# Three changes of order in a two-layer graph kernel: later loads of x and of the diagonal, other ticks for the projections, scatters without pacing copies

## The chip, the core and the metric

The kernel runs on one core of one Trainium2 chip. Five engines share the work: TensorE (PE in the profile, its weight loads PEld), VectorE (DVE), ScalarE (ACT), GpSimd (POOL) and SyncE (SP, which issues most DMAs). Each engine [...]waits on semaphores of the others. The metric is the device time of one execution in microseconds (us); lower is better.

## What is computed

The input is a batch of 16 graphs of 1024 nodes with 128 features each, and a symmetric 0/1 adjacency. Layer 0 is a masked attention, layer 1 three rounds of a graph convolution on a thinned ("dilated") adjacency. Cut to what matters:

```python
h = jnp.maximum(_layernorm(x), 0)                    # layer 0
v, q, k = relu(h @ Wv.T + bv), relu(h @ Wq.T + bq), relu(h @ Wk.T + bk)
logits = (q @ k.T) * adj - NEG * (1 - adj)
x = x + relu((softmax(logits) @ v) @ Wo.T + bo)
h = jnp.maximum(_layernorm(x), 0)                    # layer 1
adj_d = _dilate(adj, nodemask)                       # row by row, each row's removals affect later rows
h1 = _bn(relu(_sage(h,  adj_d, Wr1, Wx1, b1)))       # _sage: (adj_d @ x / deg) @ Wr + x @ Wx + b, row-normalised
h2 = _bn(relu(_sage(h1, adj_d, Wr2, Wx2, b2)))       # _bn: statistics over all graphs and nodes
h3 = _bn(relu(_sage(h2, adj_d, Wr3, Wx3, b3)))
x = x + concat(h1, h2, h3) @ Wl + bl
```

## The kernel before, in words

**Attention stage.** One step for each of the 16 graphs. A step has 48 ticks (TICKS, L35); a tick is a little over 1 us. The function step(i) (L893) issues 16 score blocks of 128 x 512 (scores, L737: PE into PSUM tile ps, ScalarE's exp into e, VectorE's product with the adjacency), each followed by two pieces of the values of the half before (values, L750: PE into po). After each piece pace() (L876) moves the tick on and advances every generator in the agenda whose next due tick has come. So everything beside the scores and values has its place in each engine's queue by a list of ticks, written by hand and counted from the step's start; plan(gen, start, ticks) (L801) enters a generator in the agenda. Clock.later (L63) puts a piece of work a given number of ticks later.

In step i the agenda holds, among others:

- load_adj(i + 1) (L820, Dilation.load L164) at AT_LOAD, ticks 1, 4, 7 and so on: eight row blocks of the next adjacency, 512 KB each, by SP into one of three st buffers (L162); ScalarE turns each into a bf16 mask ab (L174) and counts its zeros (L191). A row block takes two of the ticks, so the blocks stand at ticks 1, 7, 13, ... in the queues. SP has nothing else to wait for and runs ahead of the ticks as soon as the st buffer of three blocks ago is free.
- project(i + 1) (L698) at AT_PROJECT (L780), a list for even and one for odd steps: moments of x (DVE and POOL), normalised rows hn (POOL, L617), transposes (PE, L627), Q, K, V (PE, L720, evicted by ScalarE at L721) and V times Wo (PE, L728, evicted by DVE). From the transposes on they all use one PSUM tile, pm, with a single buffer: each piece waits until ScalarE or DVE has emptied it of the piece before.
- in odd steps the sort and the two gathers of the dilation (ticks 27 to 47 for the most part); in groups of steps its solve.
- store(i - 1) (L769, L829) from tick 75 on, so in the step after the next boundary: eight scatters of 128 rows of the new x to DRAM by POOL (scatter, L571). Odd and even steps differ in when POOL comes to them.

Two things stand outside the agenda: at the head of step i the loop at L917 issues load_x(i + 2) (L691: 512 KB by SP at L695 into one of five xt buffers, and a small DVE copy at L696 into a column of the same buffer) and dil.read_diagonal(i) (L222: 1024 single elements by SP, used by the final verdict only). The xt buffer that load_x(i + 2) takes is that of graph i - 3, whose scatters were issued in step i - 1. In step 0 the loads are in the agenda (first_loads, L885).

**Layer 1.** Rounds one and two keep their results in SBUF (r1, r2). Round three (from L1305) computes for each graph a tile y of 1024 rows of 256 numbers: the round's output (mix, L1029) and the sum of the two earlier thirds with x (thirds, L1327, added by DVE at L1131). Five graphs (STAY: 2, 5, 8, 11, 14) stay in SBUF; the rows of the other eleven are scattered to DRAM by POOL in the order of the nodes (scatter_rows, L1337: eight scatters each, 88 in all) and read back by SP (load_back, L1321). y comes from a pool of three buffers (L1305); a buffer can be used again when its scatters have landed. The scatters wait in a list, and pace_scatters (L1295), called after each of the eight pieces of a graph, puts at most one of them into POOL's queue:

```python
if ticks3 % 6 and waiting and waiting[0][0] <= ticks3:
    if marked:
        nc.gpsimd.tensor_copy(mark, last[0])
    waiting.pop(0)[1]()
```

last[0] is one column of whatever DVE last had to write in program order (a norm, batch statistics, y or z), so a scatter doesn't start before DVE has come that far. The last stage (the final product and the output, from L1433 on) has marked off and uses the same pace_scatters for its 40 scatters of the output.

Of the kernel before, what the change touches and what calls it, by code (L numbers as in the profile page):

```python
# [16 lines left out]
B, N, D = 16, 1024, 128  # L17
# [17 lines left out]
TICKS = 6 * NB  # L35
# [14 lines left out]
def _advance(gen, n=1):  # L50
    for _ in range(n):
        if next(gen, gen) is gen:
            return False
    return True
# [491 lines left out]
def fast(ctx: ExitStack, tc: tile.TileContext, a, out, vp):  # L546
# [31 lines left out]
    def load_const(name, shape, src):  # L578
        t = consts.tile(shape, F32, name=name)
        nc.sync.dma_start(t, src)  # L580
        return t

    def column(name):
        return load_const("c_" + name, [P, 1], a[name].rearrange("(p o) -> p o", o=1))

    def row_all(name):
        ap = a[name]
        return load_const("r_" + name, [P, P], bass.AP(tensor=ap.tensor, offset=ap.offset, ap=[[0, P], [1, P]]))
# [94 lines left out]
    with ExitStack() as s1:  # L683
        att = s1.enter_context(tc.tile_pool(name="att", bufs=2))
        aps = s1.enter_context(tc.tile_pool(name="aps", bufs=2, space=PSUM))
        dil = Dilation(tc, adj, accT, kept, jp, identf, dpool, dpsum,
                       rows.enter_context(tc.tile_pool(name="adj", bufs=2, side="right")), aps, clock)
# [3 lines left out]
        def load_x(b):  # L691
            X[b] = xpool.tile([P, NB, XW], F32, name="xt")
            for k in range(0, NB, NB if b else NB // 2):
                k = slice(k, k + (NB if b else NB // 2))
                nc.sync.dma_start(X[b][:, k, :D], x_in[b].rearrange("(k p) d -> p k d", p=P)[:, k])  # L695
            nc.vector.tensor_copy(X[b][:, :, D].bitcast(I32), dil.node32)  # L696
# [40 lines left out]
        def scores(b, g, k):  # L737

            p = aps.tile([P, 512], F32, name="ps")
            c = slice(512 * g, 512 * g + 512)  # L740
            nc.tensor.matmul(p, K[b][:, k * P:(k + 1) * P], Q[b][:, c], start=True, stop=True)  # L741
            e = att.tile([P, 512], F32, name="e", bufs=16)
            later(1, lambda: nc.scalar.activation(e, p, AF.Exp))  # L743
            later(2, lambda: nc.vector.tensor_mul(e, e, AB_[b][:, k, c]))  # L744
            return e
# [4 lines left out]
        def values(b, g, E, i, part):  # L750

            q = 4 * g + i
            if q % 2 == 0 and part == 0:
                pairs[b] = aps.tile([P, 2, D + 1], F32, name="po")
            po = pairs[b]
            for k in range(2 * part, 2 * part + 2):
                nc.tensor.matmul(po[:, q % 2, :], E[k][:, i * P:(i + 1) * P], V[b][:, k, :], start=(k == 0),  # L757
                                 stop=(k == NB - 1))
            if part < 3 or q % 2 == 0:
                return  # L760
            o = att.tile([P, 2, D], F32, name="o")
            rec = recips[:, b, q - 1:q + 1]
            x = X[b][:, q - 1:q + 1, :D]
            later(1, lambda: nc.vector.reciprocal(rec, po[:, :, D]))  # L764
            for h in range(2):
                later(2 + h, lambda h=h: nc.scalar.activation(o[:, h, :], po[:, h, :D], AF.Relu, scale=rec[:, h:h + 1]))  # L766
            later(5, lambda: nc.vector.tensor_add(x, x, o))

        def store(b):  # L769
            for k in range(NB):  # L770
# [6 lines left out]

        every = lambda first, n, by: [first + by * j for j in range(n)]

        AT_PROJECT = [m + every(m[4] + hn, 4, 1) + every(m[4] + wait, 10, 3)  # L780
                      for m, hn, wait in (([1, 2, 4, 7, 13], 4, 17), ([0, 1, 3, 5, 6], 4, 18))]
        AT_LOAD = every(1, 2 * NB, 3)
        AT_BOUND = [[0] + [first + by * (j // 2) + j % 2 for j in range(2 * NB)] for first, by in ((2, 5), (3, 3))]
        AT_MIRRORS = ([5, 10, 20, 25, 30, 35, 40, 44], [13, 16, 19, 22, 25, 29, 33, 41])
# [16 lines left out]
        def plan(gen, start, ticks):  # L801
            agenda.append((gen, [start + t for t in ticks]))
# [4 lines left out]
        def plan_step(i):  # L807

            start, odd = i * TICKS, i % 2
            if i == 0:  # L810

                late = lambda ticks: [TICKS // 2 + t // 2 for t in ticks]
                plan(values0, start, [3, 6, 9, 12])
            else:
                late = lambda ticks: ticks
            plan(dil.bound(i), start, AT_BOUND[odd] if i else [25, 28, 29, 30, 31, 33, 34, 35, 36, 38, 39, 40, 41, 43, 44, 45, 46])
            plan(dil.mirrors(i), start, AT_MIRRORS[odd] if i else [6, 9, 12, 15, 18, 21, 25, 28])
            if i + 1 < B:
                plan(project(i + 1), start, AT_PROJECT[odd] if i else [14, 16, 18, 20, 21, 23, 24, 25, 26, 32, 34, 36, 38, 40, 42, 43, 45, 46, 47])
                plan(load_adj(i + 1), start, AT_LOAD if i else [23, 24, 25, 27, 28, 30, 31, 32, 34, 35, 37, 38, 39, 41, 42, 44])  # L820
            if odd:
                plan(dil.sort(i - 1), start, AT_SORT)
                for b, ticks in zip((i - 1, i), LAST_GATHER if i == B - 1 else AT_GATHER):
                    gathering[b] = dil.gather(b, spare if b == B - 2 else None)
                    plan(gathering[b], start, ticks)
            if i:
                last = i == B - 1
                plan(norms_of_x2(i - 1, att), start, LAST_NORMS if last else AT_NORMS[odd])
                plan(store(i - 1), start, LAST_STORE if last else AT_STORE)  # L829
            for b0, b1, t0, t1 in GROUPS:  # L830
                if t0 // TICKS == i:
                    n = solve_pieces(b0, b1)
                    plan(dil.solve(b0, b1), 0, [t0 + j * (t1 - t0) // n for j in range(n)])
# [3 lines left out]
        def load_adj(b):  # L837
            g = dil.load(b)
            next(g)
            AB_[b] = dil.A[b][0]  # L840
            yield
            yield from g
# [33 lines left out]
        def pace():  # L876
            nonlocal tick
            clock.tick()
            for gen, ticks in agenda:
                while ticks and ticks[0] <= tick:  # L880
                    ticks.pop(0)
                    _advance(gen)
            tick += 1

        def first_loads():  # L885
            load_x(1)
            yield
            load_x(2)
            yield
            dil.read_diagonal(0)  # L890
            yield

        def step(i):  # L893
            nonlocal prev
            if i == 0:
                plan(first_loads(), 0, [1, 20, 26])
            plan_step(i)
            for g in range(2):
                E = []
                for k in range(NB):  # L900
                    E.append(scores(i, g, k))
                    if i == 0 and g == 0:
                        _advance(first, 2)
                    pace()
                    for h in range(2):
                        if prev:
                            values(*prev, k // 2, k % 2 * 2 + h)
                        pace()
                prev = (i, g, E)
# [3 lines left out]
        def load_x2(b):  # L913
            XT[b] = xpool.tile([P, NB, XW], F32, name="xt")
            nc.sync.dma_start(XT[b], x2_d[b].rearrange("(k p) d -> p k d", p=P))

        for i in range(B):  # L917
            if 0 < i < B - 2:
                load_x(i + 2)
            if i == B - 1:  # L920
                load_x2(0)
                load_x2(1)
            if i:
                dil.read_diagonal(i)
            step(i)
            if i == 0:
                wr = [load_const(f"wr{k}", [P, P], a[f"L1_gnn_Wr{k}"]) for k in (1, 2, 3)]
                wx = [load_const(f"wx{k}", [P, P], a[f"L1_gnn_Wx{k}"]) for k in (1, 2, 3)]
                gs = [column(f"L1_gnn_g{k}") for k in (1, 2, 3)]
                bes = [column(f"L1_gnn_be{k}") for k in (1, 2, 3)]  # L930
                wl = load_const("wl", [P, 3, P], a["L1_gnn_Wl"].rearrange("(k p) e -> p k e", p=P))
                below, shares, place, cols = selectors()
                bs = [row_all(f"L1_gnn_b{k}") for k in (1, 2, 3)]
                bl = row_all("L1_gnn_bl")
                for r in bs + [bl]:
                    nc.vector.tensor_scalar(r, r, below[:, 0:1], None, op0=OP.mult)
# [294 lines left out]
    with big:  # L1231
# [58 lines left out]
        rows_r = lambda b: blocks(r2[b // 2][:, b % 2, :])  # L1290
        rows_z = lambda b: blocks(r1[b // 2][:, b % 2, :])
        mark = few.tile([P, 1], F32, name="mark")
        waiting, ticks3, marked = [], 0, True

        def pace_scatters():  # L1295

# [136 lines left out]
        marked = False  # L1433
# [591 lines left out]
```

## Time and profile before

| what | before |
|---|---|
| median of 3 runs | 1218.25 us (1217.69 to 1220.84) |
| profiled execution | 1223.52 us, span of the records 1221.7 us |
| PE busy, weight loads | 1067.6 us (87%), 826.8 us (68%) |
| DVE, ACT, POOL busy | 846.0 us (69%), 727.2 us (60%), 575.2 us (47%) |
| granted PE clock, mean | 0.961 |
| attention stage | about 20 to 768 us |
| round three | about 984 to 1132 us |
| last stage | about 1132 to 1222 us |
| mark copies (L1302) | 81, 0.20 us each |

How to read the profile: a line of the waits names the engine and line that waited, after the arrow what ended the wait, then the sum in us, how often, and the longest. A line of the timeline has start, duration, engine, line, operation, output and input tile, and in brackets the idle time of the engine just before, with what ended it; "remote" means that a semaphore ended it and no instruction that ended just then explains it. "issue" is time in which nothing is seen to be waited for. A letter q after an engine is its sequencer: for SPq, the time until a DMA was issued. Matmul records have modelled ends.

### The profile page before, as it was taken

How to read it: one execution, taken by the hardware profiler on the slowest of the kernel's cores; microseconds unless marked ns; L12 is line 12 of the kernel's file. 1: busy time of each engine (PE TensorE's matmuls, PEld its weight loads, DVE VectorE, ACT ScalarE, POOL GpSimd, SP SyncE). 2: the span in 40 equal slices, each digit the busy share in tenths (PEclk: the TensorE clock that was granted, in tenths of full speed). 3: DMA queues.
4: the chain of work that ended last, by engine and by line, in shares of the span. 5: the costliest groups of instructions: out<-in, count | busy, mean ns of one | idle time of the engine just before them, and what ended most of it. 6: DMA issues, size and time to landing. Idle time of an engine off the chain costs nothing.

```text
span 1221.7 us, 22431 instructions
## 1 busy us (share of the span) xinstructions
PE 1067.6 (87%) x7731; PEld 826.8 (68%) x7731; DVE 846.0 (69%) x2611; ACT 727.2 (60%) x1771; POOL 575.2 (47%) x1063
## 2 busy tenths in 40 slices
PE   8899989989989989989999998789779887878693
PEld 3567666766666766666666676678769877878583
DVE  7757647578867657867877988679878755556331
ACT  5677866877767767766777762468758522222120
POOL 0321742842733634554446344789401056665563
PEclk9999999999999999999999999899989999898796
DMA  7445244244344344344443421334000046665542
GB/s 233 128 145 141 86 141 145 93 141 139 99 128 140 111 131 124 119 122 118 116 131 105 126 84 38 106 82 114 19 18 1 3 145 199 186 194 164 164 144 84
DMA packets 135355, 143.77 MB, mean 118 GB/s; under 512 B 25920, under 2 KB 111296, under 8 KB 135232
## 3 DMA queue, kind: packets, MB, share of 16 engines
q1 hardware_dynamic: 123328, 111.10, 32.0%
q0 software_dynamic: 11904, 31.15, 7.8%
q8 instruction: 62, 1.02, 0.3%
q14 instruction: 61, 0.50, 0.1%
HBM read 113.71 MB, written 28.51 MB: 116 GB/s over the span
## 4 chain that ended last, share of the span: by engine, by line
PE 58%; DVE 16%; ACT 10%; issue 4%; POOL 4%; DMA 3%; another core or an unknown queue 3%; POOLq 0%; DVEq 0%; ACTq 0%
PE po L757 13%; PE ps L741 12%; PE pm L720 5%; PE po L1056 4%; PE po L1394 3%; DMA st<-in_adj_dram 3%; DVE e L744 2%; ACT e L743 2%; PE pt L1114 2%; PE pm L728 2%; PE pd L200 2%; POOL x_d L573 2%; PE pt L1332 2%; PE pt L1333 2%
## 5 line engine op out<-in xcount | busy, mean ns | idle before, releaser
L757 PEld LDWEIGHTS po<-vw,e 128*128 128x128 f32 x2048 | 270.8, 194 | 58.4 <-issue 58.2
L757 PE MATMUL po<-vw,e 128*128 128x129 f32 x2048 | 304.8, 284 | 0.0
L744 DVE TENSOR_TENSOR e<-e,ab 128x512 f32<-128x512 f32 x256 | 177.7, 694 | 156.6 <-ACT e L743 147.0
L741 PE MATMUL ps<-qT,kT 128*128 128x512 f32 x512 | 269.9, 609 | 0.6 <-ACT kT L721 0.6
L743 ACT ACTIVATE e<-ps 128x512 f32<-128x512 f32 x256 | 153.4, 600 | 94.7 <-PE ps L741 88.1
L174 ACT ACTIVATE ab<-st,d_one_k 128x1024 bf16<-128x1024 f32 x126 | 145.6, 1155 | 26.9 <-DMA st<-in_adj_dram 26.8
L573 POOL DMA_INDIRECT x_d<-xt,slot x128 | 142.9, 1116 | 39.3 <-issue 33.0
L191 ACT ACTIVATE junk<-st 128x1024 bf16<-128x1024 f32 x112 | 118.6, 1059 | 0.0
L313 POOL DMA_INDIRECT rows<-in_adj_dram,row x15 | 17.2, 1147 | 177.3 <-DVE junkv L206 82.1
L573 POOL DMA_INDIRECT y_d<-y,nodes x88 | 86.3, 981 | 22.5 <-issue 18.0
L605 POOL TENSOR_SCALAR ln_t<-ln_st 128x8 f32<-128x8 f32 x31 | 11.1, 357 | 177.4 <-DVE ln_st L598 172.2
L1072 ACT ACTIVATE sq<-po 128x512 f32<-128x512 f32 x48 | 28.5, 597 | 97.8 <-remote 39.3
L766 ACT ACTIVATE o<-po,recips 128x128 f32<-128x128 f32 x128 | 46.6, 367 | 64.1 <-DVE recips L764 59.4
L741 PEld LDWEIGHTS ps<-qT,kT 128*128 128x128 f32 x512 | 78.5, 193 | 3.6 <-ACT kT L721 1.7
L1056 PE MATMUL po<-ws,r 128*128 128x128 f32 x512 | 69.0, 277 | 3.7 <-issue 3.6
L1056 PEld LDWEIGHTS po<-ws,r 128*128 128x128 f32 x512 | 65.9, 194 | 6.3 <-issue 5.2
L617 POOL TENSOR_SCALAR hn<-xt,ln 128x128 f32<-128x128 f32 x120 | 65.0, 553 | 3.2 <-ACT e L743 1.1
L206 DVE SCALAR_TENSOR_TENSOR junkv<-pd,ab 128x64 bf16<-128x64 int32 (+7 forms) x128 | 57.4, 448 | 12.5 <-PE ps L741 6.7
L1332 PE MATMUL pt<-ws,r 128*128 128x128 f32 x224 | 48.6, 302 | 16.4 <-DVE y L1131 11.4
L728 PEld LDWEIGHTS pm<-w_L_gnn_Wo,hn 128*128 128x128 f32 x256 | 34.7, 201 | 35.2 <-ACT hn L721 22.1
L617 POOL TENSOR_SCALAR hn<-xt 128x128 f32<-128x128 f32 x112 | 54.4, 496 | 8.1 <-PE pt L627 7.2
L1131 DVE TENSOR_TENSOR r<-r,po 128x512 f32<-128x512 f32 x32 | 21.1, 685 | 52.5 <-remote 30.6
(346 smaller groups left out, 2485.5 us busy)
## 6 DMA issues: line engine op xcount, KB each, us to landing
st<-in_adj_dram SPq DMA_DIRECT2D x126, 512.0 KB
r<-y_d SPq DMA_DIRECT2D x22, 512.0 KB
xt<-x_d SPq DMA_DIRECT2D x16, 524.0 KB
x<-x_d SPq DMA_DIRECT2D x16, 512.0 KB
xt<-in_x_dram SPq DMA_DIRECT2D x15, 512.0 KB
out_dram<-r SPq DMA_DIRECT2D x11, 512.0 KB
x_d<-xt,slot POOLq DMA_INDIRECT x128
y_d<-y,nodes POOLq DMA_INDIRECT x88
```

What stands on the lines that cost most here:

```text
L174: nc.scalar.activation(ab[:, k, :], st, AF.Exp, bias=self.one_k, scale=ONE_K, accum_out=self.deg[:, b, k:k + 1])
L191: nc.scalar.activation(junk(), st, AF.Exp, scale=-ZERO_K, accum_out=zeros)
L573: d = nc.gpsimd.indirect_dma_start(out=dst, out_offset=bass.IndirectOffsetOnAxis(ap=slots, axis=0), in_=src, in_offset=None)
L617: engine.tensor_scalar(hn[:, k, :], xt[:, k, :D], minus[:, k // 2, k % 2, None], rstd[:, k // 2, k % 2, None], op0=OP.add, op1=OP.mult)
L720: nc.tensor.matmul(pp, w, hT[:, 512 * g:512 * g + 512], start=True, stop=True)
L728: nc.tensor.matmul(pp[:, k, :], vT[:, j * P:(j + 1) * P], wo, start=True, stop=True)
L741: nc.tensor.matmul(p, K[b][:, k * P:(k + 1) * P], Q[b][:, c], start=True, stop=True)
L743: later(1, lambda: nc.scalar.activation(e, p, AF.Exp))
L744: later(2, lambda: nc.vector.tensor_mul(e, e, AB_[b][:, k, c]))
L757: nc.tensor.matmul(po[:, q % 2, :], E[k][:, i * P:(i + 1) * P], V[b][:, k, :], start=(k == 0), stop=(k == NB - 1))
L1056: nc.tensor.matmul(po[:, i, :], hT[:, c:c + P], wxk, start=(i == 3), stop=False)
L1332: nc.tensor.matmul(pz[:, i, :], column(r1, b, g, i), wl0, start=True, stop=False)
```

## The change

Three edits, independent of each other.

1. load_x(i + 2) and read_diagonal(i) go from the head of the step into the agenda: a generator small_loads(i) at ticks 8 and 14 of every step from 1 on (step 0 keeps its ticks 1, 20, 26). At the last two steps, where there is no further x, tick 8 is empty.
2. AT_PROJECT spells its last ten ticks out. The list for even steps is the same as before (30, 33, ... 57). For odd steps it was 24, 27, 30, ... 51 and becomes 20, 23, 26, 29, 32, 42, 45, 48, 51, 54.
3. marked is False from the start, so round three's scatters go into POOL's queue without a copy into mark ahead of each; each waits for its own data alone.

```diff
-        AT_PROJECT = [m + every(m[4] + hn, 4, 1) + every(m[4] + wait, 10, 3)
-                      for m, hn, wait in (([1, 2, 4, 7, 13], 4, 17), ([0, 1, 3, 5, 6], 4, 18))]
+        AT_PROJECT = [m + every(m[4] + 4, 4, 1) + turned
+                      for m, turned in (([1, 2, 4, 7, 13], [30, 33, 36, 39, 42, 45, 48, 51, 54, 57]),
+                                        ([0, 1, 3, 5, 6], [20, 23, 26, 29, 32, 42, 45, 48, 51, 54]))]
...
-        def first_loads():
-            load_x(1)
-            yield
-            load_x(2)
-            yield
-            dil.read_diagonal(0)
+        def small_loads(i):
+            if i == 0:
+                load_x(1)
+                yield
+            if i + 2 < B:
+                load_x(i + 2)
+            yield
+            dil.read_diagonal(i)
             yield
 
         def step(i):
             nonlocal prev
-            if i == 0:
-                plan(first_loads(), 0, [1, 20, 26])
+            plan(small_loads(i), i * TICKS, [8, 14] if i else [1, 20, 26])
             plan_step(i)
...
         for i in range(B):
-            if 0 < i < B - 2:
-                load_x(i + 2)
             if i == B - 1:
                 load_x2(0)
                 load_x2(1)
-            if i:
-                dil.read_diagonal(i)
             step(i)
...
-        waiting, ticks3, marked = [], 0, True
+        waiting, ticks3, marked = [], 0, False
```

## The prediction, made before the result was known

> **What bounds the kernel now.** I read the waits of the attention stage first (60 to 760 us of the span), then busy time by attention step, then the timelines of one odd step's start and of one stretch of round three.
>
> Waits in 60 to 760 us (engine, line, whom it waited for: us, times, longest). First TensorE (PE), then ScalarE (ACT), then SP's own queue:
>
> ```profile
> PE pm L728 <- ACT hn L721: 16.0, 7, 3.1
> PE pm L720 <- ACT kT L721: 11.6, 10, 2.3
> PE pm L720 <- ACT qT L721: 5.4, 5, 1.5
> ```
> ```profile
> ACT ab L174 <- DMA st<-in_adj_dram: 20.5, 6, 4.1
> ```
> ```profile
> SPq L695 <- DMA x_d<-xt,slot: 78.8, 12, 17.3
> ```
>
> PE is the engine that the stage runs at; it loses 33 us to these three waits for the one-buffered PSUM tile pm, which ScalarE empties. ScalarE itself stands 20.5 us waiting for adjacency rows, and SP stands 78.8 us at the load of x, because that load overwrites a buffer that scatters of two steps ago still read. Steps 9, 10 and 11 (window, its length, PE, weight loads, DVE, ACT, POOL, clock, DMA share, GB/s):
>
> ```profile
> 436.50:486.00 49.50, 44.34 (x311) 30.71 (x310) 34.02 (x129) 34.88 (x68) 21.33 (x45) 0.97 0.48 138
> 486.00:532.30 46.30, 43.90 (x339) 31.81 (x338) 36.58 (x116) 34.07 (x70) 25.47 (x45) 1.00 0.34 104
> 532.30:584.50 52.20, 46.22 (x306) 33.07 (x306) 35.88 (x143) 34.93 (x69) 20.88 (x45) 0.93 0.48 133
> ```
>
> Odd steps are longer with about the same PE work. Steps 3, 5, 7, 9, 11, 13 take 49.1, 49.2, 50.7, 49.5, 52.2 and 47.3 us (298.0), steps 4 to 14 even take 44.6, 45.2, 44.5, 46.3, 46.6 and 45.1 (272.3): 25.7 us apart. Why, at the start of step 11: SP gets its load of x out at 530.79 (the scatters' last descriptors were written at 529.3), and only then the first rows of adjacency; ScalarE and PE stop:
>
> ```profile
> 530.79 0.38 SPq L695 DMA_DIRECT2D xt<-in_x_dram  x1
> ...
> 531.89 9.21 SPq L162 DMA_DIRECT2D st<-in_adj_dram  x4
> ```
> ```profile
> 537.41 1.15 ACT L174 ACTIVATE ab<-st,d_one_k 128x1024 bf16<-128x1024 f32 x1 [3.71 <-DMA st<-in_adj_dram]
> ```
> ```profile
> 539.76 1.87 PE L728 MATMUL pm<-w_L_gnn_Wo,hn 128*128 128x128 f32 x8 [3.01 <-ACT hn L721]
> ```
>
> Round three (about 984 to 1132 us) is bound otherwise. GpSimd (POOL) writes 88 scatters and ahead of 81 of them a copy into mark; VectorE (DVE) and ScalarE stop in bursts for 5 to 6 us, and each stop ends when POOL has run out of scatters:
>
> ```profile
> 1036.01 0.98 POOL L573 DMA_INDIRECT y_d<-y,nodes  x1 [0.16 <-issue]
> 1043.19 0.18 POOL L1302 COPY mark<-y 128x1 f32<-128x1 f32 x1 [6.20 <-DVE y L1131]
> ```
> ```profile
> 1037.98 0.69 DVE L1131 TENSOR_TENSOR y<-x,pt 128x512 f32<-128x512 f32 x1 [5.81 <-remote]
> ```
>
> The add at 1037.98 needs only matmuls whose records end at 1032.6. The trace has six signals of PE between 1037.96 and 1038.20 and none in the 7 us before: PE had run, its signals came late, and they came 1 us after POOL's last scatter (1036.99).
>
> [...] the 78.8 us are on SP, and the rows of adjacency behind are late. [...] L1332 pairs take 0.63 us after the stop at 1038.7 and 0.39 us before it; so a removed wait saves a little more than itself. [...]
>
> **The change part by part.**
>
> *Load of x at tick 8, diagonal at 14.* Nothing is added. Per step one x load (0.38 us of SP), one diagonal load (0.58 us of SP, 1024 pieces of 4 bytes) and one small DVE copy (0.17 us, L696, which waits for the same scatters) move. In SP's order the first two row loads of a step now stand ahead of the load of x, the third behind it. Their buffers come free in the step before, so they can land before tick 0. In odd steps the scatters in question end about one tick (1 us) before the step; at tick 8 the load, and the DVE copy, find them done with some 9 us to spare. Were that cover gone, DVE would stop at L696 with its queue of mask products behind it, and PE with it. Who needs x: moments in the next step, 40 ticks later; who needs the diagonal: the verdict alone. Gone: seven stops of 16.0 us on PE. What is late next at those places is PE's own stream, as at the start of even steps, where ScalarE gets its rows at once. I take 13 of 16.0 us; ends 8 and 18[...].
>
> *Projections in odd steps* (transposes at ticks 20, 23 for 24, 27; Q 26, 29 for 30, 33; K 32, 42 for 36, 39; V 45, 48 and 51, 54 for 42, 45 and 48, 51). Same instructions. The scatters of an odd step run at ticks 25 to 36 (560.19 to 570.70 in step 11). Before, pm is asked for at 27, 30, 33, 36 in them and at 39 behind them, and the longer waits L720 <- kT, qT (17.0 us in 15 in all) fall at ticks 33 to 39, where ScalarE waits for PE's late signals. Now 26, 29 and 32 lie there, then nothing for ten ticks. Earlier transposes need GpSimd's normalised rows: these end at ticks 16 to 18, with the row stop still in it, so 2 ticks of cover; without it PE would stop at L627. V ends 3 ticks later, 18 ticks before values need it. I take 6 of 17.0 us; ends 0 and 13.
>
> Check of the two: 19 us of the 25.7 us by which odd steps exceed even ones.
>
> *No copies into mark.* A paced scatter comes every 1.36 us (1034.65 to 1036.01), an unpaced one every 1.26 us (in the last stage): 81 x 0.10 = 8 us of POOL. The copies' waits for DVE, 24.4 + 3.5 + 2.3 + 1.2 = 31.4 us of POOL, go as well; the scatter then waits for its own y alone, whose last write ends at 1041.9 in the example, against 1043.86 when it started: 1.9 us per pair of batches. DVE's 4.9 us of waiting for copies go too. But POOL's time is not the sum: a period of three batches takes 29.7, 31.4, 29.8 us (1013.47, 1043.19, 1074.59, 1104.36), PE's own work in it is 3 x 7.33 = 22.0 us (1046.28 to 1053.61 for one), and 16 scatters take 20.2 us unpaced. The 8 us between are the late signals, and they last as long as POOL writes on. Shorter bursts cut them by (1.6 + 1.9) us per pair at best: 5 x 3.5 = 17 us. Against it, the copies make POOL pause when DVE stops; without them two bursts of eight join. The built order also shows y buffers going strictly three batches round (batch 4 now waits for the scatters of batch 1). The trace of before can't settle the sign; ends +16 and -17 us; I take -3.
>
> Sum: 13 + 6 + 3 = 22 us. The profiled execution took 1223.52 us, its span 1221.7 (1.8 us around it), 0.4% over the median 1218.25. Span 1199.7, with the 1.8 us 1201.5, scaled by 1218.25/1223.52: 1196 us.
>
> **Rivals.**
> - *Round three gains too* (bursts shorten): -13 - 6 - 14 = 1185. For: every stop ends 1 us after POOL does. Against: the last stage, unpaced already, is no better. Chance 0.18.
> - *Loads help, projections don't* (PE's late signals just meet another wait): -13 - 0 - 0 = 1205. For: in even steps pm is asked for among scatters too (ticks 30 to 42 in 31 to 43) and PE loses little, so scatters alone are not the cause. Against: what the odd steps have besides, sort and gather at ticks 27 to 47, is what the gap from 32 to 42 steps round. Chance 0.17.
> - *Round three spoils the gain, even*: 1218 within 0.3%. Chance 0.06.
> - *Slower: unpaced scatters hold PE's signals longer in round three.* For: in the last stage, 16 unpaced scatters (1184.45 to 1204.3), PE is busy 5.00, 3.99, 1.47, 1.44 us of each 5. If round three stops after 3 us as its second bursts do now, and goes on at that 0.29 share, PE does 3 + 5 = 8 us of work in 21.2, and a period is 21.2 + 14 = 35 us: 5 x 5 = 25 us more, 1218 - 19 + 25 = 1224. It decides from 3.8 us per pair. Against: the first POOL burst of a pair loses little, and POOL pauses by itself when y isn't ready. Chance 0.10.
> - *Forecast*: 1196, with 1189 to 1202 its own. Chance 0.49.
>
> **Numbers.** Range 1181 to 1216: low takes in 13 + 6 + 17, high the loads alone (8) with some loss in round three. About 0.3% (3.7 us) is what a measurement of this kernel can tell from no change. Faster 0.84, same 0.06, slower 0.10.
>
> **What would show it.** Right: ScalarE's L174 wait for rows near 0, L728 <- hn under 4 us, odd steps within 2 us of even ones, L720 waits halved, no L627 wait of PE. Wrong: a DVE wait at L696, or the rows late at tick 13 because the third load stands behind x. Round three: scatters every 1.26 us; the length of 970 to 1132 (162 us) and the stops marked remote tell which of the rivals holds.

## The result, and the profile after

| | before | changed |
|---|---|---|
| median of 6 runs each | 1219.9 us (1217.69 to 1221.4) | 1227.56 us (1224.35 to 1230.38) |
| profiled execution, span | 1223.52, 1221.7 us | 1226.19, 1224.4 us |
| mean granted PE clock | 0.961 | 0.947 |
| start of the span to the first scatter of round three | 986.4 us | 961.3 us (-25.1) |
| first to last scatter of round three | 156.1 us | 188.2 us (+32.1) |
| from there to the end | 79.2 us | 74.9 us (-4.3) |

The ratio is 1.0063, 95% interval 1.0044 to 1.0081: 0.6% slower, where 1196 us and faster were forecast. The sum of the three parts is +2.7 us, that of the two profiled spans; the medians are 7.7 us apart, since the profiled run of before lies 3.6 us above its median and that of the changed kernel 1.4 below. The three stretches are cut at records of the trace: the start of the first and the end of the last scatter into y_d.

The attention stage did what the change was to do there. Waits of the changed kernel from 60 to 760 us, first PE, then SP's queue:

```profile
PE pm L720 <- ACT kT L721: 2.8, 4, 0.9
...
PE pm L720 <- ACT qT L721: 0.7, 1, 0.7
...
PE pm L728 <- ACT hn L721: 0.3, 1, 0.3
```
```profile
SPq L695 <- DMA x_d<-xt,slot: 30.1, 10, 7.2
```

PE's 33.0 us at the tile pm are down to 3.8. SP still waits for the scatters at the load of x, 30.1 us instead of 78.8, but no row of adjacency is late behind it: ScalarE's wait at L174 is not in this window any more. Steps 9, 10 and 11 (window, length, then PE, weight loads, DVE, ACT, POOL busy, PE clock, DMA share, GB/s):

```profile
420.20:465.10 44.90, 44.04 (x324) 30.90 (x324) 34.06 (x126) 34.18 (x66) 21.88 (x45) 1.00 0.47 132
465.10:511.20 46.10, 43.74 (x329) 31.23 (x328) 36.41 (x115) 34.66 (x70) 25.57 (x46) 1.00 0.42 127
511.20:558.30 47.10, 43.40 (x304) 30.38 (x304) 35.22 (x143) 34.22 (x67) 21.35 (x45) 1.00 0.45 123
```

The odd steps, the first and the third line, are 44.9 and 47.1 us long instead of 49.5 and 52.2, and their clock is 1.00 instead of 0.97 and 0.93.

Round three gave it all back. Its waits and those of the last stage (970 us to the end), two lines of before and then the changed kernel, whose line numbers are two lower:

```profile
DVE r L1131 <- remote: 40.8, 7, 9.1
ACT sq L1072 <- remote: 39.3, 7, 6.7
```
```profile
DVE r L1129 <- remote: 87.3, 12, 14.3
ACT sq L1070 <- remote: 77.3, 5, 17.1
POOL y_d L573 <- DVE y L1102: 63.5, 4, 17.3
```

"Remote" is again a semaphore with no record that ended just then. The largest case, in GpSimd's timeline and below in VectorE's:

```profile
961.31 1.10 POOL L573 DMA_INDIRECT y_d<-y,nodes  x1 [31.31 <-DVE y L1102]
962.72 0.97 POOL L573 DMA_INDIRECT y_d<-y,nodes  x1 [0.30 <-issue]
...
971.59 0.96 POOL L573 DMA_INDIRECT y_d<-y,nodes  x1 [0.30 <-issue]
...
980.46 0.96 POOL L573 DMA_INDIRECT y_d<-y,nodes  x1 [0.30 <-issue]
```
```profile
966.97 0.69 DVE L1073 TENSOR_REDUCE nrm<-sq 128x4 f32<-128x512 f32 x1 [1.05 <-ACT sq L1070]
980.48 0.69 DVE L1129 TENSOR_TENSOR r<-x,pt 128x512 f32<-128x512 f32 x1 [12.82 <-remote]
```

Sixteen scatters follow each other at 1.27 us without a pause, from 961.31 to 981.4: the first graph's eight, and at 971.59 those of the second, whose y was ready meanwhile. VectorE stands for 12.82 us and goes on with the start of the sixteenth. PE's semaphore shows why: it has a signal at 964.21 and the next at 980.45, though seven matmuls with a signal have records in between, the first ended at 965.3. Busy time in the same stretch:

```profile
961.30:970.00 8.70, 8.44 (x74) 8.17 (x72) 5.23 (x11) 2.07 (x5) 6.86 (x7) 1.00 0.26 93
970.00:980.00 10.00, 0.00 (x0) 0.00 (x0) 0.00 (x0) 0.00 (x0) 7.56 (x9) 0.60 0.29 105
```

For 10 us PE, VectorE and ScalarE have no instruction to show; GpSimd goes on. All the 88 scatters now come in five runs of 16 and one of 8; before, the runs were of 2 to 8, and of 12 once. Round three as a whole, from the first to the last scatter, before and after (columns as above):

```profile
986.40:1142.50 156.10, 124.71 (x962) 118.82 (x961) 89.77 (x182) 41.16 (x95) 101.98 (x168) 0.93 0.62 182
```
```profile
961.30:1149.50 188.20, 134.31 (x956) 125.37 (x955) 88.52 (x180) 41.94 (x95) 84.91 (x88) 0.82 0.53 151
```

### The profile page after: what moved, and what is told of

Same layout as the page of the kernel before. It is cut to its first block, busy times and chain, and to the rows that moved or that the text cites. A ratio compares the mean times of both kernels' runs of the same rounds, so it can differ in the third digit from the quotient of the medians.

```text
span 1224.4 us, 22283 instructions
## 1 busy us (share of the span) xinstructions
PE 1073.7 (88%) x7731; PEld 833.2 (68%) x7731; DVE 844.4 (69%) x2611; ACT 727.7 (59%) x1771; POOL 561.4 (46%) x982
## 4 chain that ended last, share of the span: by engine, by line
PE 60%; DVE 19%; ACT 7%; issue 7%; POOL 3%; another core or an unknown queue 1%; DMA 1%; DVEq 0%; SPq 0%; POOLq 0%; ACTq 0%
PE po L757 13%; PE ps L741 12%; PE pm L720 5%; PE po L1054 5%; DVE e L744 3%; PE po L1392 3%; PE pt L1330 3%; PE pt L1112 3%; PE pt L1331 2%; PE pd L200 2%; ACT e L743 2%; DVE m L374 2%; DVE left L317 1%; DVE onehot L302 1%
## 5 line engine op out<-in xcount | busy, mean ns | idle before, releaser
L757 PEld LDWEIGHTS po<-vw,e 128*128 128x128 f32 x2048 | 266.8, 191 | 56.9 <-issue 55.5
L174 ACT ACTIVATE ab<-st,d_one_k 128x1024 bf16<-128x1024 f32 x126 | 146.2, 1160 | 5.9 <-DMA st<-in_adj_dram 5.9
L1330 PE MATMUL pt<-ws,r 128*128 128x128 f32 x224 | 50.1, 298 | 32.9 <-issue 21.4
L1330 PEld LDWEIGHTS pt<-ws,r 128*128 128x128 f32 x224 | 39.3, 208 | 36.0 <-issue 24.0
L1331 PE MATMUL pt<-ws,r 128*128 128x128 f32 x224 | 48.9, 295 | 12.1 <-issue 11.7
```

The costliest lines, as they stand in the source:

```text
L174: nc.scalar.activation(ab[:, k, :], st, AF.Exp, bias=self.one_k, scale=ONE_K, accum_out=self.deg[:, b, k:k + 1])
L1330: nc.tensor.matmul(pz[:, i, :], column(r1, b, g, i), wl0, start=True, stop=False)
L1331: nc.tensor.matmul(pz[:, i, :], column(r2, b, g, i), wl1, start=False, stop=True)
```

## The experiments

My theory after this result: each part keeps its own sign; the loads bring the attention stage's gain, and the dropped copies lose more than that, because they were a brake, which stopped GpSimd when VectorE stopped and so let PE's signals out. The rivals were that round three suffers from the phase at which it is entered, or from the three parts together. The kernels of one group below ran on one chip, beside the kernel before, and a ratio compares the two there; each group had another chip. Which chip the first measurement had is not recorded.

### One part at a time

Loads alone (first part of the diff, nothing else):

> The kernel before with the loads of x and of the diagonal at ticks 8 and 14, and nothing else. Theory (each part keeps its sign, and the attention stage's 26 us come mostly from the rows of adjacency that no longer stand behind the load of x): 1203 us (-17), ScalarE's wait at L174 for rows near 0 and PE's wait at L728 for hn under 4 us. Rival (the loads only move the stop to PE's late signals, and the projections bring the gain): 1215 or more. Second rival (the loads bring all of it): 1194.

Projections alone (second part):

> The kernel before with the odd steps' projections at the new ticks, and nothing else. Theory: 1211 us (-9), PE's waits at L720 for qT and kT halved or better, and the waits at L728 for hn and at L174 for rows as before. Rival (the projections bring most): 1200 or less. Second rival (they bring nothing by themselves, and only with early rows): 1218 to 1221.

The copies into mark dropped alone:

```diff
-        waiting, ticks3, marked = [], 0, True
+        waiting, ticks3, marked = [], 0, False
```

> The kernel before without the copies into mark, and nothing else. Theory (without the copies nothing stops GpSimd when VectorE stops, runs of 16 scatters form, and PE's signals come only at their end): 1253 us (+33), with runs of 16 scatters at 1.27 us and stops of PE's signals of 10 us or more. Rival (round three lost its time to the phase at which it was entered, or to something that the other two parts left behind): within 6 us of 1220.

Loads and projections, with the copies kept:

> The changed kernel with the copies into mark kept, so loads and projections together. Theory: 1194 us (-26), round three as long as before (162 us from 970 to 1132 of the kernel before). Rival (the phase of round three decides): 1210 or more, with stops of PE's signals of 10 us or more in spite of the copies.

| | median | of before (95%) | odd steps 3 to 13: length, PE busy, PE idle | PE clock there |
|---|---|---|---|---|
| before, on this chip | 1156.4 us | 1 | (no trace) | |
| loads | 1122.98 us | 0.9708 (0.9688 to 0.9728) | 258.7, 257.2, 1.6 us | 1.00 |
| projections | 1156.99 us | 1.0004 (0.9988 to 1.0020) | 292.7, 269.0, 23.7 us | 0.95 |
| no copies | 1151.93 us | 0.9963 (0.9948 to 0.9978) | 292.4, 270.6, 21.8 us | 0.95 |
| loads and projections | 1124.02 us | 0.9720 (0.9700 to 0.9739) | 259.3, 255.5, 3.8 us | 1.00 |

The table did not fit my numbers, nor the rival's. The kernel before took 1156.4 us on this chip, 63.5 less than where the change was measured. Dropping the copies made it 4.5 us faster, not 33 slower. Loads bring 33 us, the projections nothing. Step 9, without the loads moved (the run without copies) and with them (the loads alone):

```profile
433.90:482.00 48.10, 44.58 (x317) 31.53 (x316) 35.50 (x136) 34.97 (x68) 21.16 (x45) 0.96 0.51 145
```
```profile
412.40:454.90 42.50, 42.50 (x315) 30.35 (x315) 34.68 (x134) 34.97 (x67) 21.89 (x45) 1.00 0.50 140
```

In the waits of the projections alone, from 60 to 760 us, the late rows are all still there:

```profile
ACT ab L174 <- DMA st<-in_adj_dram: 26.8, 6, 5.8
PE pm L728 <- ACT hn L721: 20.3, 7, 4.7
...
PE pm L720 <- ACT kT L721: 0.9, 1, 0.9
PE pm L720 <- ACT qT L721: 0.7, 1, 0.7
```

What goes with the other level is in the semaphores. In the trace of the run without copies every signal of PE stands within 0.015 us of the end of its matmul; in that of the changed kernel on the first chip some 90 of 1577 matmuls with a signal have none recorded within 1 us, and the next one stands up to 15.2 us behind. Signals come late in the one measurement and not in the other. Below, "no late signals" means a trace with at most one signal of PE over 1 us behind (1.1 us).

### The changed kernel on another chip, and kinds of brakes

Four kernels: the changed kernel; the same with the copies kept; with a copy of a constant in place of the one that waits for VectorE; and with the waiting copy at the first scatter of each graph only.

> The changed kernel itself, on whichever chip this call gets. The kernel before took 1220 us where the change was measured and 1156 us on the chip of the four runs of single parts, where no trace has a signal of PE that is late. Theory (late signals under GpSimd's scatters come with the chip; the loads gain on both, the dropped copies lose only where signals come late): if the kernel before takes about 1156 us here, then 1120 (0.969 of before) and no late signals; if it takes about 1220, then 1228 (1.006) and stops of PE's signals of 10 us or more. Rival (the three parts together do what none does alone: the later loads put round three into the phase in which runs of 16 scatters hurt): 1.00 to 1.01 of before on either chip.

> The changed kernel with the copies into mark kept, beside the changed kernel on the same chip. Theory: where the kernel before takes about 1156 us, 1124 (0.972), 4 us above the changed kernel; where it takes about 1220, 1194 (0.979), 34 us below the changed kernel. Rival (the parts work on each other): 0.972 on either chip is not reached where signals are late, 1215 or more.

```diff
-        waiting, ticks3, marked = [], 0, False
+        waiting, ticks3, marked = [], 0, True
...
-                    nc.gpsimd.tensor_copy(mark, last[0])
+                    nc.gpsimd.tensor_copy(mark, eps)
```

> The changed kernel with 81 copies into mark of a constant column: the same GpSimd instruction ahead of each scatter, without the wait for VectorE. Theory (the copies help as a brake, by stopping GpSimd when VectorE stops): on a chip with late signals as long as the changed kernel, 1228, with runs of 16 scatters; where no signal is late 1122, 2 to 3 us above the changed kernel, for 8 us more of GpSimd. Rival (the copies help by the 0.1 us that they put between scatters): 1194 on a chip with late signals, as with the marks kept.

```diff
-        waiting, ticks3, marked = [], 0, False
+        waiting, ticks3, marked, issued = [], 0, True, 0
...
+                issued += 1
-                if marked:
+                if marked and issued % 8 == 1:
                     nc.gpsimd.tensor_copy(mark, last[0])
```

> The changed kernel with the copy into mark (with its wait for VectorE) ahead of every eighth scatter only, the first of each graph. Theory (runs of 16 are the harm; one brake a graph cuts them to 8): on a chip with late signals 1200 to 1210, runs of 8 scatters, no stop of PE's signals over 11 us; where no signal is late 1121, as the changed kernel. Rival (any unpaced run hurts as much as a long one): 1225 or more on a chip with late signals.

| before 1155.73 us | median | of before (95%) | first to last scatter |
|---|---|---|---|
| changed | 1121.81 us | 0.9719 (0.9688 to 0.9749) | 117.0 us |
| copies kept | 1124.77 us | 0.9742 (0.9713 to 0.9772) | 121.0 us |
| copies of a constant | 1123.97 us | 0.9736 (0.9706 to 0.9767) | 120.2 us |
| one waiting copy a graph | 1131.22 us | 0.9798 (0.9767 to 0.9828) | 127.6 us |

No late signals here either, and the changed kernel is 2.8% faster than before. At the head of round three its scatters follow each other without a pause too, 32 of them; beside the first 16 (940.3 to 960.3):

```profile
940.30:950.30 10.00, 9.95 (x89) 9.93 (x89) 7.78 (x18) 4.04 (x10) 7.79 (x8) 1.00 0.33 98
950.30:960.30 10.00, 9.90 (x86) 9.85 (x87) 7.36 (x14) 3.14 (x7) 7.64 (x8) 1.00 0.94 286
```

PE is busy 9.9 of 10 us beside the scatters that stopped it altogether on the first chip. So a run of 16 scatters is no harm by itself. The rival of the three parts together is out: it asked for 1.00 to 1.01 on any chip, and all three together took 0.9719, near the product of the parts, 0.9708 x 1.0004 x 0.9963 = 0.968.

The one waiting copy a graph cost 9.4 us against the changed kernel, where I had expected nothing. Its waits from 940 to 1075 us:

```profile
DVE y L1129 <- DMA y_d<-y,nodes: 16.7, 7, 4.5
...
POOL mark L1301 <- DVE y L1129: 13.8, 4, 4.0
```

My reading: GpSimd waits at the copy until VectorE has come to that point of the program, all eight scatters of the graph start later for it, and VectorE then waits for these scatters to get its y buffer back (the first line; 8.5 us in the changed kernel). It is not shown, since the kernel with all copies kept waits at the first scatter of a graph too and took 121.0 us. One copy a graph wasn't run on a chip with late signals.

### Which of the loads, and the best of the parts

The load of x alone at tick 8, the diagonal left at the head of the step; and both loads moved, no copies, old projections.

> The kernel before with the load of x alone at tick 8; the load of the diagonal stays at the head of the step, the projections and the copies into mark as before. Theory (the rows of adjacency stood behind the load of x, which waits for scatters; the load of the diagonal waits for nothing): as with both loads moved, 0.971 of the kernel before, PE idle in odd steps 3 to 13 under 5 us in all. Rival (the diagonal's 1024 pieces of 4 bytes hold the rows back as well): 0.985 or more. On a chip with late signals of PE both stand some 8 us nearer to the kernel before.

> The changed kernel with the old ticks for the projections: both loads moved, no copies into mark. Theory (the projections' ticks are worth nothing once the rows come early): where the kernel before takes about 1156 us, 1119 to 1122 (0.969), 3 us below the loads alone; where it takes about 1220 and signals come late, 1225 to 1232. Rival (the three parts hang together): more than 4 us off the changed kernel's 0.972 where no signal is late.

Before 1157.6 us; x alone 1124.38 us, 0.9707 (0.9686 to 0.9729), PE idle 1.2 us in the odd steps. The diagonal has no part in it. Loads without copies and without the projections: 1119.88 us, 0.9675 (0.9656 to 0.9694), the fastest kernel of those that leave nothing out. It was run on a chip without late signals only.

### Stores in place of scatters

```diff
-                for k in range(NB):
-                    waiting.append((ticks3 + 2, lambda k=k: scatter(y_d[b], nodes[:, b, k:k + 1], y[:, k, :], f"y_{b}")))
+                later(2, lambda: nc.sync.dma_start(y_d[b].rearrange("(k p) d -> p k d", p=P), y))
```

> The changed kernel with each graph's eight scatters of round three replaced by one store of the whole tile y by SP, in the graph's own order of rows: it leaves out the reordering of the rows, and writes the same 1 MB. Theory: on a chip with late signals of PE they come late only while GpSimd issues scatters, so round three has no stop of PE's signals over 2 us and takes 110 to 125 us where the changed kernel took 188: about 1160 in all. Where no signal is late, GpSimd's 88 scatters at 1.27 us (112 us) and PE's own work (105 of 110 us) are nearly level, and the kernel gains 0 to 8 us on the changed kernel. Rival (late signals come from the amount of data moved, not from GpSimd's issuing): the stops stay where they were, 1215 or more.

> The changed kernel itself once more, beside the run with plain stores, on whichever chip this call gets. Theory (the chip decides): 0.970 of the kernel before with no late signals if the kernel before takes about 1156 us here, 1.006 with stops of 10 us and more if it takes about 1220. Rival (something other than the chip made the difference between the first measurement and the later ones): any other pair, such as 0.97 beside 1220.

Again no late signals. Before 1156.06 us; stores 1119.76 us, 0.9700 (0.9671 to 0.9728); changed 1122.67 us, 0.9719 (0.9691 to 0.9748). Where signals come in time, round three has little to gain without GpSimd (2.9 us here). The question that the stores were made for stayed open, and so it did when they were run a second time, beside the loads alone:

> The changed kernel with one store of y by SP in place of each graph's eight scatters in round three, again; it leaves out the reordering of the rows. Theory (signals are late only while GpSimd issues scatters): on a chip with late signals 0.945 to 0.955 of the kernel before (about 1160 where that takes 1222), no signal of PE more than 2 us late in round three, which takes 110 to 125 us; in the last stage, which keeps its 40 scatters, late signals as before. Rival (the amount of data moved makes them late): 0.98 or more. Where no signal is late: 0.970, as it was.

> The kernel before with the two loads moved and nothing else, for a chip with late signals, where loads and projections together took 0.974 of the kernel before and odd steps 3 to 13 took 267.5 us against 298.0. Theory (the projections bring a little there, since they ask for their PSUM tile outside of the scatters): odd steps 270 to 274 us, 0.977 to 0.980. Rival (they bring nothing there either): 266 to 269 us, 0.974.

Before 1155.86 us; stores 1118.88 us, 0.9676 (0.9660 to 0.9693); loads 1123.24 us, 0.9709 (0.9693 to 0.9726). No late signals.

### Two chips with late signals

Small loads beside the scatters of the changed kernel, and the changed kernel with its copies kept:

```diff
+            if ticks3 <= 128:
+                for j in range(4 * ticks3 - 4, 4 * ticks3):
+                    r = slice(j % 32 * 4, j % 32 * 4 + 4)
+                    nc.sync.dma_start(dots[r, j // 32:j // 32 + 1], x_in[0, r, j // 32:j // 32 + 1])
             if ticks3 % 6 and waiting and waiting[0][0] <= ticks3:
```

> The changed kernel with four loads of four single numbers each by SP at every tick of the first 128 of round three, 512 in all, into a column nobody reads: more landings, and more semaphore increments of DMA engines, beside GpSimd's scatters. Theory[...]: signals of PE later than 1 us appear in the first half of round three also on a chip that has none, and the kernel gains 10 us or more on the changed kernel's time. Rival (they are a trait of the first chip, or of its state, that this doesn't touch): PE's signals stay at 0.015 us, and the time is within 6 us of the changed kernel's 0.972 of before.

> The changed kernel with the copies into mark kept, once more, on whichever chip this call gets. Theory: 0.973 of the kernel before where that takes about 1156 us and no signal is late; about 1194 (0.979) where it takes about 1220 and signals come late, since round three then keeps its 156 us from first to last scatter and the attention stage its gain. Rival: 1215 or more on a chip with late signals.

This chip had late signals: before took 1225.07 us. With the copies kept 1191.3 us, 0.9740 (0.9667 to 0.9813), 3 us from the 1194 expected. Another such chip had the small loads again and the copies of a constant:

> The changed kernel with the 512 small loads again, for a chip of the other kind. On the chip with late signals it took 1262.7 us, some 35 above the changed kernel's 1228, with round three's scatters spread over 224 us against 188. Theory[...]: where the kernel before takes about 1156 us, within 6 us of the changed kernel (1116 to 1130), signals at 0.015 us. Rival (the small loads cost their time on SP's queue, ahead of the loads of x and of the rows read back, and this would be so on any chip): 1140 or more.

> The changed kernel with copies of a constant column ahead of the scatters (no wait for VectorE), for a chip with late signals. Theory (the copies help as a brake): 1.00 to 1.01 of the kernel before on such a chip, round three's scatters spread over 180 us or more, runs of 16. Rival (they help by the 0.1 us between scatters): 0.974 and 151 us, as with the copies kept. Where no signal is late, 0.9736 of before, as it was.

Before 1220.32 us; copies of a constant 1219.23 us, 1.0002 (0.9980 to 1.0023). Round three, from the first to the last scatter, in the trace with the copies kept and then in that with copies of a constant:

```profile
957.80:1109.10 151.30, 126.69 (x956) 120.04 (x955) 89.51 (x181) 41.08 (x95) 102.22 (x168) 0.91 0.63 188
```
```profile
961.70:1142.30 180.60, 144.43 (x954) 129.43 (x953) 89.04 (x180) 41.56 (x95) 102.17 (x168) 0.79 0.54 157
```

Both have the same 168 instructions on GpSimd in this stretch and the same time between scatters (1.36 us); they differ in what the copies wait for. With the wait round three takes 151 us, with the scatters in runs of 1 to 8 and one of 12; without it 181, in five runs of 16 (two of them with a short gap inside) and one of 8. PE is idle 36.2 us (180.60 - 144.43) instead of 24.6, and busy 17.7 us longer on the same work, at a clock of 0.79 instead of 0.91. So the copies help by their wait, as the theory has it, and not by the time between scatters. (The two ran on different chips with late signals, 0.9740 and 1.0002 of the kernel before on each.)

The small loads took 1262.67 us (1.0306, 1.0237 to 1.0375) and 1264.86 us (1.0379, 1.0293 to 1.0465), round three 224 us both times. They don't settle what more landings do to PE's signals, since they also stood in SP's queue ahead of the loads of x. Waits in the first of the two traces, 955 to 1190 us:

```profile
DVE y L1129 <- DMA x<-x_d: 56.0, 7, 11.6
...
DVE r L1129 <- DMA x<-x_d: 39.0, 4, 13.3
```

No run of them on a chip without late signals is on record, which would have told.

## Why the prediction was wrong

**Loads: mechanism right, 13 us mis-sized.** The loads of x alone bring 33 us where no signal is late. On the first chip, loads and projections together shortened odd steps 3 to 13 from 298.0 to 269.7 us, by 28.3 where the sum had 19. I had added up seven named waits of PE (16.0 us) and called it all. The line to take was PE's idle time of the odd steps as a whole, 31.5 us against 11.6 after: -19.9. The other 8.4 us of the 28.3 are PE's busy time, 266.6 against 258.1, since the clock was 0.973 there and is 1.00 now. The record of the granted clock shows it: between 60 and 700 us before stood at 0.5 five times for 3.4 us, each time in an odd step, and the changed kernel never. In a stretch of that kind in round three of before (1038.4 to 1041.8 us) PE's pairs at L1332 take 0.63 us, against 0.39 ahead of it. At 0.5, 5 x 3.4 us come to some 8.5 us lost, my estimate from that record; my "a little more than itself" was too little. My check of the sum against the 25.7 us between odd and even steps was no ceiling either: odd steps are shorter than even ones now, 45.0 us in the mean against 45.6. The stated checks held: no late rows at tick 13, no wait of DVE at L696, no wait of PE for GpSimd's rows at L627 in the window.

**Projections: 6 us forecast, nothing found where it could be tried.** 1.0004 alone, and on top of the loads no gain: 0.9720 with them and 0.9708 without, 0.9719 and 0.9675 where the copies are dropped too, so rather a loss of up to 0.4%, which these intervals don't settle. The waits at L720 that I meant to halve were themselves late signals: on a chip without these they are 1.2 and 1.5 us with the old ticks (the loads alone, twice). On the chip of the first measurement they went from 17.0 to 3.5 us; which of the two edits did that stays open, for the loads alone were not run on a chip with late signals.

**Round three: the step that failed.** "The trace of before can't settle the sign; ends +16 and -17 us; I take -3." This term, the price of the dropped copies, had the wrong sign on the chip of the prediction: +32.1 us from the first to the last scatter. Where no signal is late, -3.0 and -4.5 us were measured (1121.81 against 1124.77 with overlapping intervals, 1151.93 against 1156.4). That is luck and no support for the -3, which was picked between two ends and reasoned from late signals that aren't there. The rival that I gave 0.10, unpaced scatters holding PE's signals longer, named the place and the cause, and its price, 25 us, came near. My two sentences against it failed. "The first POOL burst of a pair loses little" was true (PE is busy 8.44 of 8.70 us beside it) and beside the point: it is followed by 10 us in which PE does nothing, where the rival's sum had let PE go on at a share of 0.29. "POOL pauses by itself when y isn't ready": before VectorE stops it has finished the next graph's y, so the second eight follow without a pause and the stop goes on. 88 scatters are 5.5 pairs; 32.1 / 5.5 = 5.8 us a pair, beyond the 3.8 from which I had said that it decides. In the sum, PE's idle time in round three went from 31.4 to 53.9 us and its busy time from 124.7 to 134.3 on the same work, at a clock of 0.82 instead of 0.93: the granted clock was 0.5 for five stretches of 13.7 us, one begun in each run of 16, where before had six of 3.4 us. I had also named the brake, the copies that make GpSimd pause when VectorE stops, and given it no number.

**What made the choice look even.** I set a saving of GpSimd's time against an unknown; but with PE's signals late, GpSimd was not what round three waited for, and the longest stops ended only when it paused. That could be read from the trace of before: in round three the five longest delays of PE's signals (4.2 to 6.0 us) end 0.9 to 1.0 us after the last scatter of a run, while delays of 1 to 3.2 us ended within runs too.

**Shown, and not shown.** Shown: the loads' gain alone where no signal is late, and together with the projections on a chip with late signals, 0.974 with the copies kept; the harm of the dropped copies only where signals are late; that the copies help by their wait. That this wait works by pausing GpSimd while VectorE stops is argued from the traces. Late signals belong to GpSimd's scatters and gathers in time: of the 113 that are over 1 us late in the trace of before, all are of matmuls that ended in a run of these or within 0.4 us of its end, and of the 1034 signals that come over 3 us after the last of these none is late. The amount of data alone doesn't account for it: between 60 and 760 us of that trace the DMAs moved some 137 GB/s in the stretches that these 1034 signals stand in, and 87 in the others. Whether the issuing by GpSimd or the kind of transfer holds the signals is not shown, since the plain stores met no such chip; nor is it shown whether more landings beside the scatters make the signals later, since the small loads held up SP's queue (VectorE waited 56.0 + 39.0 us for the loads of x behind them). Why three measurements show late signals and five don't is open.

## What to carry to other kernels

An instruction that looks like pure overhead may be a brake (round three took 151 us with the copies that wait and 181 with copies that don't, where signals are late); before it is dropped, ask what its wait stops, and who gets through in the pause. Size a queue's late load by the idle time and the lost clock of the whole stage behind it: here these were 19.9 and 8.4 us (loads and projections together), and the waits that I had added up 16.0. Where before and after are compared on one chip, look whether the trace has stops that end with "remote": the changed kernel took 1.0063 of the kernel before where they were and 0.9719 where no signal was late, and loads and projections moved with the copies kept is the version measured to gain on both (0.974 and 0.972 to 0.974).

## What the runs showed of the hardware that was not expected

The same program, the kernel before, took 1220 to 1225 us where the change was first measured and in two of the groups, and 1156 to 1158 in the five others. With loads and projections moved and the copies kept, the two kinds are 64.1 us of span apart (1185.8 and 1121.7): 15.6 up to round three's first scatter, 30.9 from there to the last, 17.6 after it. So half of it lies in the 150 us in which GpSimd scatters most, and in the last stage 40 scatters took 61 us against 50.2. No chip is on record twice, so whether this is a trait of the chip or a state that it was in is not shown. A second mark of the first kind: of the first of eight semaphores that count landings of scatters the traces of kernels that issue all scatters hold 150 to 199 events there, 543 to 547 in the others. The semaphores of ScalarE and VectorE lack events as well (1090 and 1824 in the first trace of the changed kernel, 1178 and 1975 in the second). Some of these are only not recorded: ScalarE's sq ends at 1071.93, the trace has no event of its semaphore from 1068.08 to 1073.10, and VectorE's reduction that waits for it starts at 1071.97. So a part of the signals counted as late may be lost records; the stops marked remote are real, and in the traces with late signals all of them are VectorE's and ScalarE's, none PE's.
